# Counting edges behind the samples on ScalarE as sums of signs, and clamping keys on GpSimd, in a graph network on one Trainium2 core

## Chip, cores and metric

The program runs on one core of one Trainium2 chip. A core has five engines that work side by side and wait for each other by semaphores: TensorE (PE; its weight loads are listed as PEld), VectorE (DVE), ScalarE (ACT), GpSimd (POOL) and SyncE (SP), which here issues transfers. The metric is the device time of one execution in microseconds, the median of several. Before the change three runs took 1608.21, 1609.29 and 1603.38 us.

## The reference

Two graph networks follow each other on 6250 nodes with 64 features and 200,000 edges, sorted by destination. Cut to what matters:

```
msg  = x[src]
agg  = segment_sum(msg, dst);  cnt = segment_sum(1, dst)
h    = relu(agg / max(cnt, 1) @ W_l1.T + b_l1 + x @ W_r1.T)
...                                    # the same again with W_l2, b_l2, W_r2
x    = layernorm(x + out)
# three message layers; every node also has an edge to itself with attributes 1
m    = concat([h[dst], h[src], edge_attr]) @ W.T + b
h    = relu(segment_sum(m, dst))       # batch norm and relu after the first two
x    = layernorm(x + h)
```

The destinations are 6250 * u^2 of a uniform u, so low nodes have many more edges than high ones. Each segment sum over gathered rows is a product with the matrix A, where A[d, s] is the number of edges from s to d.

## The kernel before

**Stages.** The kernel builds A once, as 13 tiles of 512 destinations (`TW`) against 6272 padded sources, one byte per element. It multiplies with it in five layers: the first layer while A is being built, and later the second layer and the three message layers, for which the tiles come back from memory. The building takes about the first 540 us of the span. Then come the edge attributes together with the second layer, then the message layers.

**Slots.** A plan made from the expected distribution cuts each tile of A into windows of 1 to 10 destinations and gives each window a number of slots, 2569 in all. A slot is a list of up to 128 edges, one per partition in the product. 128 slots make one row tile t; there are 21 of them. For row tile t the kernel needs the first edge of each of its slots (`start_i[:, t]`, one slot per partition). `fetch(t)` then reads 128 consecutive edges for each slot by two indirect DMAs on the GpSimd queue, one for dst and one for src, into the tile `rows`.

**Keys.** `columns(t)` (lines 900 to 917) turns rows into keys. VectorE takes src >> 7 (L905), combines dst * 49 + (src >> 7) (L906) and src mod 128 (L907), subtracts the first key of the slot's window and takes the minimum with 2000 (L908, the clamp). PE transposes both keys (L913), so that edges lie on partitions and slots along the free dimension, and ScalarE copies them to 16 bits as `k2` (L915). The key of an edge outside the window matches nothing.

**One-hots.** For each 16 slots VectorE writes a one-hot tile `lo` of src mod 128 (128x2048), and for each run of slots a one-hot tile `rhs` of the first key (up to 128x2048). Both are made by the tensor_tensor of L628, which compares `iota` with `k2`, both in SBUF. The pool `hot` holds three buffers of each. PE multiplies lo and rhs slot by slot into PSUM (L1012, tile `pair`, two buffers) and ScalarE writes the finished windows to A as bytes (L1019, L1024). The first layer of a finished tile (`first_layer`; its products are at L666) runs on PE between and beside these products.

**Finding the first edges.** dst is sorted and sampled at every 400th edge (`GAP`); 125 x 4 samples lie in SBUF. The row tiles are searched in five groups (`SEARCH`): tile 0, tiles 1 to 4, 5 to 10, 11 to 15, and 16 to 21; column 21 holds the starts for the attributes. For a group, `near_samples` (L830 to L838) counts the samples below each slot's first destination by a compare on VectorE and a product with ones on PE. `gather_behind` (L843) reads for each row tile of the group the 400 destinations behind the last such sample, one slot per partition, by one indirect DMA on the GpSimd queue into one of six buffers `blks`. `first_edges` (L847 to L864) counts how many of the 400 are below the slot's first destination. This is one tensor_scalar with an accumulator per row tile on VectorE (L852), whose elementwise result `junk` nobody reads. Three more small VectorE instructions for the group (L854, L855, L864) make `start_i` of the counts.

**Order.** `on_slot` (L919 to L950) sets the order of this work within the building loop. At the start of row tile t (slot 32 of tile 0) come `first_edges` of a group whose turn it is (groups 1 to 4 at tiles 0, 2, 4, 6), then `fetch(t + 1)`, then `near_samples` and `gather_behind` of a later group (groups 2 to 4 at tiles 1, 3, 5; group 1 stands before the loop). In the middle of tile t (slot 64; 96 in tile 0) comes `columns(t + 1)`. Instructions marked `pin` keep this order among themselves on their engine. The others are placed by the scheduler of the language by priority and by a model of when their inputs are ready, which is why one-hots stand between the steps of a search on VectorE. Each engine then works through its list in order, and an instruction that waits holds up all that stand behind it on its engine.

GpSimd's list during the building is short: the indirect DMAs of `fetch` (42) and `gather_behind` (22), which it issues itself, and a few memsets. The indirect DMAs of `fetch(t + 1)` can be issued once `start_i` is there and the columns of tile t - 1 have read their buffer of rows, of which there are two.

Of the kernel before, what the change touches and what calls it, by code (L numbers as in the profile page):

```python
# [16 lines left out]
AF = mybir.ActivationFunctionType  # L17
ALU = mybir.AluOpType
# [456 lines left out]
def gnn_kernel(ctx: ExitStack, tc: tile.TileContext, x, src, dst, ea, W_l1, b_l1, W_r1, W_l2, b_l2, W_r2,  # L475
# [10 lines left out]
    nc = tc.nc  # L486
    pin = tc.keep_in_program_order
# [9 lines left out]
    GAP = EC1 // NSMP  # L497
# [26 lines left out]
    c_np = np.zeros((P, 3, R + 1), np.float32)  # L524
# [9 lines left out]
    for i, (b, c, g) in enumerate(subs):  # L534
        e_np[:, 0, i] = E - g * P
        e_np[:, 1, i] = np.arange(P) * g
        e_np[:, 2, i] = b * P
    c_dram = nc.inline_tensor(c_np, name="slot_table")
    e_dram = nc.inline_tensor(e_np, name="attr_table")
    t_dram = nc.inline_tensor(t_np, name="first_edges")  # L540
# [6 lines left out]
    with ExitStack() as fast:  # L547
# [203 lines left out]
        with ExitStack() as bld:  # L751
            ep = bld.enter_context(tc.tile_pool(name="edge", bufs=1))
            tab = ep.tile([P, 3, R + 1], F32, name="tab")
# [16 lines left out]
            most = max(min(b, R + 1) - a for a, b, *_ in SEARCH)  # L770
# [7 lines left out]
            def spare(n):  # L778
                k = free[0].shape[1] - n
                t, free[0] = free[0][:, k:], free[0][:, :k]  # L780
                return t
# [33 lines left out]
            blks = [spare(GAP).bitcast(I32) for _ in range(most)]  # L815
            junk = spare(GAP // 2).bitcast(BF16)
# [5 lines left out]
            c2 = pp.tile([P, R + 1], F32, name="c2")  # L822
# [24 lines left out]
            def first_edges(g):  # L847

                t0, t1 = SEARCH[g][0], min(SEARCH[g][1], R + 1)
                s = slice(t0, t1)  # L850
                for t in range(t0, t1):
                    pin(nc.vector.tensor_scalar(junk, blks[t % most], tab[:, 0, t: t + 1], None,  # L852
                                                ALU.is_lt, ALU.add, accum_out=c2[:, t: t + 1]))
                nc.vector.scalar_tensor_tensor(near[:, s], near[:, s], float(GAP), c2[:, s], ALU.mult, ALU.add)  # L854
                nc.vector.tensor_add(near[:, s], near[:, s], tab[:, 1, s])  # L855
                if g == 0:


                    nc.vector.tensor_single_scalar(near[:, R: R + 1], near[:, s], float(E - P), ALU.min)
                    nc.vector.tensor_copy(start_i[:, s], near[:, R: R + 1])  # L860
                    nc.vector.tensor_sub(near[:, s], near[:, s], near[:, R: R + 1])
                    nc.vector.tensor_scalar(passed, iota[:, :P], near[:, s], 4000.0, ALU.is_lt, ALU.mult)
                else:
                    pin(nc.vector.tensor_copy(start_i[:, s], near[:, s]))  # L864
# [35 lines left out]
            def columns(t):  # L900

                rows = fetched.pop(t)
                hi = ew.tile([P, P], I32, name="hi", bufs=1)
                key = ew.tile([P, 2, P], F32, name="key")
                pin(nc.vector.tensor_single_scalar(hi, rows[:, 1, :], 7, ALU.logical_shift_right))  # L905
                nc.vector.scalar_tensor_tensor(key[:, 0, :], rows[:, 0, :], float(NB), hi, ALU.mult, ALU.add)  # L906
                nc.vector.scalar_tensor_tensor(key[:, 1, :], hi, -float(P), rows[:, 1, :], ALU.mult, ALU.add)  # L907
                nc.vector.tensor_scalar(key[:, 0, :], key[:, 0, :], tab[:, 2, t: t + 1], 2000.0, ALU.subtract, ALU.min)  # L908
                if t == 0:
                    nc.vector.tensor_add(key[:, 0, :], key[:, 0, :], passed)  # L910
                kp = psm.tile([P, 2, P], F32, name="lin")
                for i in range(2):
                    nc.tensor.transpose(kp[:, i, :], key[:, i, :], ident)  # L913
                k2 = ew.tile([P, 2, P, 2], F16, name="k2")
                nc.scalar.copy(k2, kp.unsqueeze(3).to_broadcast([P, 2, P, 2]))  # L915
                cols[t] = k2, {}
                cols.pop(t - 2, None)

            def on_slot(slot):  # L919

                t, c = divmod(slot, P)
                if c == (32 if t == 0 else 0):
                    for g, (*_, t1) in enumerate(SEARCH):
                        if t == t1:
                            first_edges(g)
                            if g == len(SEARCH) - 1:
                                first_attributes()
                    if t + 1 < R:
                        fetch(t + 1)
                    for g, (_, _, t0, _) in enumerate(SEARCH):  # L930
                        if t == t0:
                            near_samples(g)
                            gather_behind(g)
                    gather_dst(t)
                if c == (96 if t == 0 else 64) and t + 1 < R:
                    columns(t + 1)
                    if t == 0:
                        for to, of in early_weights:
                            transposed(to, of)
# [13 lines left out]
            gather_behind(0)  # L953
            near_samples(1)
            first_edges(0)
            fetch(0)
            gather_behind(1)
            columns(0)
            load_x()
            pin(nc.sync.dma_start(thr[:, early:], t_ap[:, early:].to_broadcast([EP, P * (R + 1) - early])))  # L960
# [331 lines left out]
```

## Time and profile before

The profile shows one execution. Its own time was 1605.75 us, of which the span from the program's first instruction to its last is 1604.0 us. The mean granted clock of TensorE was 0.977.

| engine | busy, us | share of the span |
|---|---|---|
| PE | 1488.1 | 93% |
| PEld | 1370.7 | 85% |
| DVE | 905.4 | 56% |
| ACT | 575.4 | 36% |
| POOL | 217.7 | 14% |

The groups of instructions around the change:

| line, engine | what | count | us of one |
|---|---|---|---|
| L852 DVE | count among 128x400, int32 to bf16, with accumulator | 22 | 0.62 |
| L908 DVE | subtract and minimum on 128x128 f32 | 21 | 0.28 |
| L906, L907 DVE | the two keys | 21 each | 0.29 |
| L628 DVE | one-hots rhs (240) and lo (161) | 401 | 1.02 and 1.22 |
| L843 POOL | indirect DMA into blks | 22 | 0.94 to 10.95 |
| L896 POOL | indirect DMA into rows | 42 | 0.94 to 22.88 |
| L1019 ACT | evacuation of pair | 355 | 0.90 |

How to read the profile: busy times are those of the whole span, while the engines are busy in different stages, so a stage is judged by the slices and windows of that stage. The chain of waits is followed back from the last instruction, at each step to what released it. "Idle before" is the time for which an engine stood still ahead of a group, with what ended most of it. For an indirect DMA the record on POOL is the time in which GpSimd issues it, not that of the transfer, which lands later.

### The profile page before, as it was taken

Reading aid. Unit: us, or ns where it says so; the run is one execution under the profiler, and the core shown is the slowest. Engines: PE = TensorE matmul, PEld = TensorE weight load, DVE = VectorE, ACT = ScalarE, POOL = GpSimd, SP = SyncE. Lnnn points to the kernel's source line nnn. Section 1 sums busy time; section 2 is a strip of 40 time slices with the busy share of each in tenths; the row PEclk is TensorE's granted clock in tenths of the full one; section 3 lists DMA queues with packets and bytes.
Section 4 is the critical chain, followed back from the end, with each engine's and each line's share of the span. In section 5 each row is a group of like instructions: output and inputs, shape, how many; then the busy total and the mean of one; then the engine's idle time right before and its main releaser. Section 6 shows DMA issues by size and latency. Waiting matters only on the chain.

```text
span 1604.0 us, 38502 instructions
## 1 busy us (share of the span) xinstructions
PE 1488.1 (93%) x17115; PEld 1370.7 (85%) x17115; DVE 905.4 (56%) x1499; ACT 575.4 (36%) x1086; POOL 217.7 (14%) x93
## 2 busy tenths in 40 slices
PE   3887799999998999999999999999899999999997
PEld 2666688888886898899899989889799999899997
DVE  5899998988968509987986511111431112442222
ACT  2737476777848404544553200000310000310000
POOL 2465830731601100000000000000000000000000
PEclk9898999999999999999999999999899999899998
DMA  5302232320421536435344354443345444164540
GB/s 135 125 29 96 46 100 88 154 99 4 169 85 71 226 160 243 174 131 200 135 146 148 135 241 161 162 171 122 132 167 220 177 175 168 81 247 173 197 163 11
DMA packets 45200, 227.32 MB, mean 142 GB/s; under 512 B 23621, under 2 KB 31650, under 8 KB 37343
## 3 DMA queue, kind: packets, MB, share of 16 engines
q1 hardware_dynamic: 37965, 139.40, 23.1%
q10 hardware_dynamic: 4306, 78.10, 12.4%
q0 software_dynamic: 2752, 7.26, 1.6%
q8 instruction: 136, 2.23, 0.5%
q14 instruction: 41, 0.34, 0.1%
HBM read 183.77 MB, written 42.57 MB: 141 GB/s over the span
## 4 chain that ended last, share of the span: by engine, by line
PE 65%; DVE 17%; issue 7%; ACT 6%; DMA 3%; POOL 2%; ACTq 0%; DVEq 0%; POOLq 0%
PE agg L666 49%; PE pair L1012 7%; DVE lo L628 6%; ACT a L1019 3%; DVE rhs L628 2%; PE u L1166 2%; POOL parts L843 2%; DVE e L1070 2%; PE bank L1079 1%; DVE z L693 1%; DMA e<-in_edge_attr_dram 1%; DVE e L1072 1%; PE lin L1188 1%; PE tr L718 1%; PE lin L740 1%
## 5 line engine op out<-in xcount | busy, mean ns | idle before, releaser
L666 PE MATMUL agg<-parts,a 128*128 128x192 bf16 (+1 forms) x12005 | 1088.2, 247 | 4.4 <-DVE parts L649 1.3
L666 PEld LDWEIGHTS <-a 128*128 128x128 fp8e3 x12005 | 1006.4, 98 | 30.5 <-issue 19.6
L1019 ACT ACTIVATE a<-pair 128x784 fp8e3<-128x784 f32 (+3 forms) x355 | 294.2, 900 | 106.2 <-PE pair L1012 90.4
L1012 PE MATMUL pair<-rhs,lo 128*128 128x147 bf16 (+5 forms) x2569 | 259.4, 237 | 43.7 <-ACT a L1019 17.0
L1012 PEld LDWEIGHTS <-lo 128*128 128x128 bf16 x2569 | 191.6, 100 | 97.6 <-issue 49.2
L628 DVE TENSOR_TENSOR rhs<-iota,k 128x1960 bf16<-128x1960 f16 (+15 forms) x240 | 239.5, 1020 | 18.5 <-ACT k L915 10.5
L628 DVE TENSOR_TENSOR lo<-iota,k 128x2048 bf16<-128x2048 f16 x161 | 195.7, 1220 | 1.9 <-ACT k L915 1.3
L693 DVE TENSOR_REDUCE z<-agg 128x256 f32<-128x768 f32 (+1 forms) x39 | 35.3, 910 | 271.8 <-PE agg L666 271.4
L896 POOL DMA_INDIRECT rows<-ends,start_i x40 | 140.4, 3510 | 180.3 <-DVE key L908 154.1
L628 DVE TENSOR_TENSOR lo<-iota,e_d 128x2048 bf16<-128x2048 f16 (+11 forms) x132 | 130.9, 1012 | 19.6 <-PE bank L1079 17.6
L1079 PE MATMUL bank<-lo,lhs 128*128 128x128 bf16 x1701 | 107.6, 219 | 17.6 <-ACT lhs L1073 12.4
L1079 PEld LDWEIGHTS <-lhs 128*128 128x128 bf16 x1701 | 98.3, 98 | 29.1 <-ACT lhs L1073 20.4
L693 DVE TENSOR_REDUCE nd<-agg 128x256 f32<-128x768 f32 (+1 forms) x26 | 23.5, 907 | 116.5 <-PE agg L666 110.8
L1182 POOL TENSOR_TENSOR nd<-res,inv 128x256 f32<-128x256 f32 (+1 forms) x13 | 7.6, 588 | 550.2 <-DVE z L1128 341.2
L720 ACT COPY mx<-tr 128x512 f32<-128x512 f32 (+1 forms) x26 | 14.7, 566 | 169.7 <-PE tr L718 169.6
L709 ACT ACTIVATE sp_r<-z 128x256 f32<-128x256 f32 (+1 forms) x26 | 10.5, 403 | 172.2 <-DVE z L708 172.0
L1206 ACT ACTIVATE hr<-hr 64x512 f32<-64x512 f32 (+1 forms) x13 | 7.9, 605 | 172.2 <-DVE hr L1205 172.2
L843 POOL DMA_INDIRECT parts<-in_dst_dram,pos x22 | 53.9, 2448 | 41.0 <-DVE pos L838 31.6
L1069 ACT CAST lhs<-e 128x512 bf16<-128x512 f32 (+21 forms) x72 | 36.1, 503 | 64.0 <-PE bank L1079 43.4
L1070 DVE TENSOR_TENSOR e<-e,lhs 128x512 f32<-128x512 f32 (+21 forms) x72 | 39.5, 552 | 14.9 <-ACT lhs L1069 14.7
L1191 DVE TENSOR_SCALAR ext<-lin 64x512 f32<-64x512 f32 (+1 forms) x13 | 8.6, 663 | 68.5 <-ACT hr L1189 68.5
L1073 ACT CAST lhs<-e 128x512 bf16<-128x512 f32 (+21 forms) x72 | 36.4, 505 | 23.1 <-DVE e L1072 22.6
(149 smaller groups left out, 816.4 us busy)
## 6 DMA issues: line engine op xcount, KB each, us to landing
a<-adj SPq DMA_DIRECT2D x24, 3136.0 KB
a<-adj ACTq DMA_DIRECT2D x24, 3136.0 KB
adj<-a SPq DMA_DIRECT2D x12, 3136.0 KB
e<-in_edge_attr_dram SPq DMA_DIRECT2D x25, 256.0 KB
a<-adj SPq DMA_DIRECT2D x4, 784.0 KB
out_dram<-z SPq DMA_DIRECT2D x12, 128.0 KB
e<-in_edge_attr_dram SPq DMA_DIRECT2D x7, 152.0 KB
adj<-a SPq DMA_DIRECT2D x1, 784.0 KB
```

What stands on the lines that cost most here:

```text
L628: nc.vector.tensor_tensor(to.rearrange("p g (h two) -> p g h two", two=2), iota[:, :n].rearrange("p (h two) -> p h two", two=2).unsqueeze( ...
L666: nc.tensor.matmul(sums[k][:, i, :n], views[k][:, b, i * P: (i + 1) * P], pt[:, b, :n], start=(b == sources[0] and terms is None and not ( ...
L693: nc.vector.tensor_reduce(to, ps[:, :nb, : 3 * D].rearrange("p b (r d) -> p b d r", r=3), AX.X, ALU.add)
L843: pin(nc.gpsimd.indirect_dma_start(out=blks[t % most], out_offset=None, in_=dst.rearrange("(e o) -> e o", o=1), in_offset=bass.IndirectOff ...
L896: pin(nc.gpsimd.indirect_dma_start(out=rows[:, i, :], out_offset=None, in_=end, in_offset=bass.IndirectOffsetOnAxis(ap=start_i[:, t: t + 1 ...
L1012: nc.tensor.matmul(pair[:, bank % 2, col: col + wc], lo_hot(t, c), rhs[:, i, :wc], start=first, stop=last)
L1019: nc.scalar.activation(av[:, :, o: o + 2 * nd].rearrange("p h (two d) -> p h two d", two=2), pair[:, :, : nd * NB].rearrange("p two (d h) ...
L1069: nc.scalar.copy(lhs[:, :g, 0:EC], r)
L1070: nc.vector.tensor_sub(r, r, lhs[:, :g, 0:EC])
L1073: nc.scalar.copy(lhs[:, :g, 2 * EC:3 * EC], r)
L1079: nc.tensor.matmul(ps[:, :P], lhs[:, q, :], oh[:, q % HOT, :], start=(c == 0 and q == 0), stop=(i == last_b[b] and q == g - 1))
L1166: pin(nc.tensor.matmul(u[:, i, :], y[:, i * P: (i + 1) * P], maps[n - 1], start=True, stop=True))
```

## The change

In `first_edges` the counts of groups 1 to 4 (21 instructions) move from VectorE to ScalarE. ScalarE has no compare with a sum, so it takes the sign of (threshold - destination) for each of the 400 destinations and accumulates the signs. To keep the difference from ever being zero, the thresholds in the table `c_np[:, 0]` are lowered by 0.5. The sum is (number below) - (number above), so (sum + 400) / 2 is the count, and one more VectorE instruction per group makes it. Group 0 keeps its count on VectorE.

In `columns` the clamp of the first key moves from VectorE to GpSimd for all row tiles but tile 0 (20 instructions). It now stands on GpSimd between VectorE's L906 and PE's transposes.

```diff
@@ -535,6 +535,7 @@
         e_np[:, 2, i] = b * P
+    c_np[:, 0] -= 0.5
     c_dram = nc.inline_tensor(c_np, name="slot_table")
...
@@ -849,8 +850,15 @@
                 for t in range(t0, t1):
-                    pin(nc.vector.tensor_scalar(junk, blks[t % most], tab[:, 0, t: t + 1], None,
-                                                ALU.is_lt, ALU.add, accum_out=c2[:, t: t + 1]))
+                    if g == 0:
+                        pin(nc.vector.tensor_scalar(junk, blks[t % most], tab[:, 0, t: t + 1], None,
+                                                    ALU.is_lt, ALU.add, accum_out=c2[:, t: t + 1]))
+                    else:
+
+                        pin(nc.scalar.activation(junk, blks[t % most], AF.Sign, bias=tab[:, 0, t: t + 1], scale=-1.0,
+                                                 accum_out=c2[:, t: t + 1]))
+                if g:
+                    nc.vector.tensor_scalar(c2[:, s], c2[:, s], float(GAP), 0.5, ALU.add, ALU.mult)
                 nc.vector.scalar_tensor_tensor(near[:, s], near[:, s], float(GAP), c2[:, s], ALU.mult, ALU.add)
...
@@ -905,7 +913,7 @@
                 nc.vector.scalar_tensor_tensor(key[:, 1, :], hi, -float(P), rows[:, 1, :], ALU.mult, ALU.add)
-                nc.vector.tensor_scalar(key[:, 0, :], key[:, 0, :], tab[:, 2, t: t + 1], 2000.0, ALU.subtract, ALU.min)
+                (nc.gpsimd if t else nc.vector).tensor_scalar(key[:, 0, :], key[:, 0, :], tab[:, 2, t: t + 1], 2000.0, ALU.subtract, ALU.min)
                 if t == 0:
```

## The prediction

> **What bounds the kernel now.** I read the page first: its slices of 40 us, then the chain of waits.
>
> ```profile
> PE   3887799999998999999999999999899999999997
> ...
> DVE  5899998988968509987986511111431112442222
> ...
> PE 65%; DVE 17%; issue 7%; ACT 6%; DMA 3%; POOL 2%; ACTq 0%; DVEq 0%; POOLq 0%
> ```
>
> TensorE sets the end over most of the span, but not everywhere: in slices 1 to 4 (40 to 200 us) PE reads 8877 and DVE 8999. The change touches only the building of adjacency tiles, which fills these slices, so I cut them into windows of 20 us.
>
> ```profile
> core 0: us, PE busy (x) PEld busy (x) DVE busy (x) ACT busy (x) POOL busy (x), PEclk, DMA share, GB/s
> ...
> 80.00:100.00 20.00, 19.67 (x302) 17.21 (x300) 20.00 (x35) 4.05 (x6) 6.79 (x2) 1.00 0.01 3
> 100.00:120.00 20.00, 14.53 (x124) 10.31 (x123) 20.00 (x34) 8.14 (x16) 18.01 (x7) 0.91 0.18 55
> 120.00:140.00 20.00, 13.10 (x149) 9.40 (x147) 19.89 (x30) 19.22 (x25) 2.69 (x2) 1.00 0.04 11
> ```
>
> DVE is full from about 60 to 210 us. There a microsecond off VectorE's queue is a microsecond off the end, as long as PE's idle time lasts: windows 20 to 200 us hold 141.7 us of PE in 180, so about 38 us can be won at most. From 200 to 440 us PE is busy 231.6 of 240 us and hides small VectorE savings.
>
> **What VectorE gets rid of.** The timeline of DVE around the first moved count:
>
> ```profile
> 30.28 0.62 DVE L852 TENSOR_SCALAR_CACHE_REDUCE parts<-parts,tab 128x400 bf16<-128x400 int32 x1
> 30.83 0.08 DVE L852 DVE_READ_ACCUMULATOR parts<-parts,tab 128x1 f32 x1
> 30.83 1.22 DVE L628 TENSOR_TENSOR lo<-iota,k 128x2048 bf16<-128x2048 f16 x1
> ```
>
> A count costs 0.55 us from start to start. 22 counts less the one of group 0 leaves 21: 21 x 0.55 = 11.6 us, all between 30 and 169 us. The clamp L908 costs 0.20 from start to start (48.02 to 48.22). 20 move, 4.0 us; ten of them (tiles 2 to 9, 12, 16) stand where DVE has no gap, 2.0 us; the rest was hidden behind PE. DVE also waited 1.34 us at 159.33 for a gather; that wait goes to ACT. Added: four small tensor_scalars on c2, 0.07 each by L837 (58.16 to 58.23), 0.3. Gain 11.6 + 2.0 + 1.3 - 0.3 = **14.6 us**.
>
> **What ScalarE gets.** No row shows a Sign or an accumulator on ACT. The nearest with a bias are L742 (678 ns at 512 from PSUM) and L1163 (759 at 512, bias and scale). At 0.9 ns an element, the slope between L1024 at 490 elements (0.58) and at 392 (two in 0.98, 0.49 each), 400 elements are 0.58 to 0.66; with DVE's 0.08 for the accumulator about 0.7, so 21 x 0.7 = 15 us. ACT is 53% busy from 60 to 200 us and PE waits only 7.9 us for its evacuations L1019, so I take 2 us, ends 0 and 10. If Sign needs its own table, each group pays two loads of 1.28 us (the row of L915): 0 to 10 us, I take 0. Queued behind a Sign that waits for its gather are the evacuations of pair, and PE behind them. In group 1 the extra c2 step lengthens the way to start_i by one hop (36.89 to 38.04 to 39.25): 1 us, ends -3 and 3, the gain being that ACT may count earlier.
>
> **What GpSimd gets.** Free of others it is cheap, L552 being the nearest row, against 0.28 on DVE. The chance of it being free is what decides. Timelines of POOL and of DVE:
>
> ```profile
> 1.95 0.54 POOL L552 TENSOR_SCALAR minus<-ident 128x128 bf16<-128x128 f32 x1
> ...
> 59.80 1.61 POOL L843 DMA_INDIRECT parts<-in_dst_dram,pos  x1 [12.55 <-DVE pos L838]
> ...
> 95.23 9.20 POOL L843 DMA_INDIRECT parts<-in_dst_dram,pos  x1 [0.29 <-DVE pos L838]
> 104.73 7.76 POOL L843 DMA_INDIRECT parts<-in_dst_dram,pos  x1 [0.30 <-issue]
> ...
> 141.92 10.95 POOL L843 DMA_INDIRECT parts<-in_dst_dram,pos  x1 [18.77 <-DVE pos L838]
> ...
> 235.25 1.88 POOL L896 DMA_INDIRECT rows<-ends,start_i  x1 [14.25 <-DVE key L908]
> ...
> 291.26 22.88 POOL L896 DMA_INDIRECT rows<-ends,start_i  x1 [20.93 <-DVE key L908]
> ```
>
> ```profile
> 103.51 0.29 DVE L908 TENSOR_SCALAR key<-key,tab 128x128 f32<-128x128 f32 x1
> ...
> 151.96 0.29 DVE L908 TENSOR_SCALAR key<-key,tab 128x128 f32<-128x128 f32 x1
> ...
> 313.23 0.29 DVE L908 TENSOR_SCALAR key<-key,tab 128x128 f32<-128x128 f32 x1
> ```
>
> The same gather takes 0.94 us on a quiet chip and up to 22.88 while DVE runs one-hots back to back. It is not the DMA: three of the long ones end at 104.43, 152.87 and 314.14, each 0.91 to 0.92 us after the start of a **DVE clamp**, as if begun only then; 173.16 and 401.91 do the same (clamps at 188.36, 416.23). Others end after a count, a read of PSUM (L729) or a gap. So POOL's read of SBUF is shut out by the one-hots (two SBUF inputs), and what let it in were the counts and clamps that the change takes off VectorE. At 59.80 and 235.25 the wait was one one-hot only, so it is not certain each time.
>
> The Trainium skill ("SBUF — State Buffer", § Who interferes with whom) says that a VectorE instruction with two SBUF inputs contends with a GpSimd instruction that reads SBUF, and that the second to issue blocks until the first has finished. Taken literally that is one one-hot, at most 1.2 us a clamp, hidden behind the finished one-hots, which gives the first rival's time; this trace shows 22 us across some 18 one-hots, and I go by the trace.
>
> Who waits for the clamp? PE's two transposes L913, in order, with all later matmuls behind them. From the end of the clamp to the transposes tiles 1, 2, 4, 5, 7 and 16 have 0.06 us, and 3, 8, 9, 12 and 20 under 0.9; 6, 10, 11, 13 to 15 and 17 to 19 have 2.3 to 15.1, which hides the move (where it is gone, the price is that of a plain tile below). A shut-out clamp is released when DVE runs out of lo and rhs buffers (3 each); by the ends of the matmuls that last read them they are free about 4 us before they are written again, from 80 to 140 us. Then DVE idles for clamp 0.54, a hop 0.15 (48.29 to 48.35 is 0.06, taken twice and rounded up), transposes 0.44 and 10 to 13 matmuls of 0.1 until a buffer is free, 1.3: **2.5 us**.
> - Plain tiles 1, 3, 5, 7, 8, 9, 12, 16, 20: ends 0 and 2.5 each. After one stall PE runs late and the next key is early for it, so I take half: 9 x 1.2 = 11 (0 to 22).
> - Tiles 2, 4, 6: the clamp of tile t+1 stands on POOL behind the 6, 5 and 6 gathers issued at tile t's start, 1.25 apart when free (18.20 to 19.45), and behind fetches whose rows are early enough. Tile 2: gathers end at 68.19, key was at 66.55: 2.5. Tile 4: gather one is shut out as at 95.23, five follow in DVE's idle time, 5 x 1.25 + 2.5 = 8.8. Tile 6: 6 x 1.25 + 2.5 = 10, less 2.3 slack, 8. Together 19 (0 if let in, 25).
>
> A granted POOL instruction can hold VectorE in turn:
>
> ```profile
> 480.86 5.33 POOL L979 MEMSET a<- 128x6272 int32 x1 [32.94 <-PE pair L1012]
> ...
> 481.73 4.48 DVE L730 TENSOR_SCALAR inv<-cnt 128x4 f32<-128x4 f32 x1
> ```
>
> L730 is 0.16 elsewhere. A clamp let in early may so cost DVE its 0.54 for the 0.20 saved, 10 x 0.3 = 3 us in the rival; in the forecast it runs while DVE is idle.
>
> **Sum.** The profiled execution took 1605.75 us (span 1604.0 and 1.75 around it), 2.5 below the median 1608.21 and inside the runs' 1603.38 to 1609.29; I start from it. -14.6 + 11 + 19 + 2 + 1 = +18: **1624 us**.
>
> **Rivals.** *POOL is let in at the next boundary* (59.80, 235.25 speak for it; the five ends on L908 against): no stall, gain 14.6, less 3 held DVE and 1 to 3 for ACT and the chain: 1595. It decides as soon as the clamp waits under about 4 us, DVE's lead in buffers, and the gathers are through before it. *Gain and stalls cancel*: clamps get in, but the gathers of tiles 4 and 6 still stand in front, 14.6 - 3 against 12 to 14: 1606. For it: these gathers were slow already. *ACT becomes the bound* (19.22 of 20 at 120 to 140 us): table loads 10 and blocked evacuations 10 instead of 2, on top of the forecast: 1642. Against it: ACT idles 106 us before L1019.
>
> **How the numbers follow.** Forecast 0.56, let in 0.26, cancel 0.12, ACT 0.06. A measurement here tells about 0.5% from no change, so faster is below 1600, slower above 1616. The forecast's own range is 1610 (no plain stall, gathers 19) to 1650 (22 + 25 + 10 for ACT + 3 for the chain), each less 14.6; but for its lowest edge, which I leave with it, it is slower: slower 0.62, same 0.12, faster 0.26. The range reaches down past 1595 to 1591, the lower ends, and up to 1650: 1591 to 1650.
>
> **What would show it.** POOL clamps with a median over 1 us and some over 4; waits of L913's transposes for the key (5.4 us before) of 20 us or more, then named POOL; DVE gaps of 2 us or more before L628, released by PE, between 80 and 210 us; gaps of 8 us near the gathers of tiles 4 and 6. Wrong if clamps stay near 0.5 us, if POOL runs them ahead of the gathers, or if DVE has no gaps and the spans shift left by 10 us at 210. A table load next to each Sign would show the third rival.

## Result and the profile after

The change makes the kernel slower: 1647.5 us in the median of four runs, against 1605.8 us in four runs of the kernel before, a ratio of 1.027 (95% interval 1.024 to 1.030). That is about 42 us more, where the prediction had 18 more. The direction came as predicted, GpSimd's read is shut out as predicted, and the time lies in the range (1591 to 1650). What such a wait costs was priced wrongly, and the gathers and the gain were mis-sized too.

The profiled execution took 1645.6 us with a span of 1643.7, 39.7 more than before. The change puts eight lines into the kernel, so the clamp is L916 after, the transposes L921, the fetch L904, the Sign L858, the one-hots L629 and the products of slots L1020. First the slices of 40 us, the chain and the group of the clamp, all of the kernel after:

```profile
PE   3677789899898889999999999999899999999997
DVE  5779978997877723997888721111341211441222
PE 53%; DVE 10%; issue 4%; DMA 3%; ACT 3%; POOL 1%; SPq 0%; ACTq 0%; POOLq 0%; DVEq 0%
L916 POOL TENSOR_SCALAR key<-key,tab 128x128 f32<-128x128 f32 x20 | 62.9, 3145 | 299.3 <-DVE key L914 236.2
```

VectorE is less full in slices 1, 2 and 5, counted from 0 as in the prediction (7, 7 and 7; before 8, 9 and 9), as if it had been relieved. But PE is less full there too (6, 7 and 8; before 8, 8 and 9). The clamp, 0.28 us on VectorE, takes 3.1 us in the mean on GpSimd. PE's waits during the building show who pays; first the kernel before (20 to 540 us), then the kernel after (20 to 577 us, where its building ends). The columns are the total, the number of waits and the longest:

```profile
PE pair L1012 <- ACT a L1019: 17.0, 46, 0.7
PE pair L1012 <- DVE lo L628: 12.8, 20, 2.1
PE pair L1012 <- DVE rhs L628: 7.5, 14, 1.1
PE lin L913 <- DVE key L908: 2.2, 1, 2.2
```

```profile
PE lin L921 <- POOL key L916: 40.8, 11, 6.0
PE pair L1020 <- ACT a L1027: 19.0, 45, 1.4
PE pair L1020 <- DVE lo L629: 7.0, 9, 2.1
PE pair L1020 <- DVE rhs L629: 4.5, 7, 2.0
```

PE waits 8.8 us less for one-hots (20.3 to 11.5) and 38.6 us more for keys. One of these waits in full, tile 8, in the timelines of VectorE, of GpSimd and of PE's weight loads after:

```profile
197.92 0.28 DVE L915 SCALAR_TENSOR_TENSOR key<-hi,rows 128x128 f32<-128x128 int32 x1
198.13 1.15 DVE L629 TENSOR_TENSOR rhs<-iota,k 128x1924 bf16<-128x1924 f16 x1
199.20 1.22 DVE L629 TENSOR_TENSOR lo<-iota,k 128x2048 bf16<-128x2048 f16 x1
200.33 1.16 DVE L629 TENSOR_TENSOR rhs<-iota,k 128x1924 bf16<-128x1924 f16 x1
201.40 1.22 DVE L629 TENSOR_TENSOR lo<-iota,k 128x2048 bf16<-128x2048 f16 x1
204.48 0.24 DVE L629 TENSOR_TENSOR rhs<-iota,k 128x148 bf16<-128x148 f16 x1 [1.86 <-PE pair L1020]
```

```profile
198.18 5.03 POOL L916 TENSOR_SCALAR key<-key,tab 128x128 f32<-128x128 f32 x1 [13.67 <-DVE key L914]
```

```profile
203.26 0.29 PEld L921 LDWEIGHTS lin<-ident,key 128*128 128x128 f32 x2 [5.03 <-POOL key L916]
```

The clamp's record starts at 198.18. VectorE makes four more one-hots, until its buffers are full, and the last one ends at 202.62. The clamp ends 0.59 us later, at 203.21, and PE goes on at 203.26, having stood for 5.03 us. VectorE itself stood for 1.86. So **PE loses the whole time in which VectorE fills its buffers, not only VectorE's own pause after it**: the one-hots made meanwhile belong to products that stand behind the transposes in PE's list.

The building ends at 576.6 instead of 539.9, 36.7 us later. PE's busy time up to there grows by 7.2 of these (466.3 to 473.5), and its idle time by the other 29.5. The granted clock of the stretch falls from 0.96 to 0.93, and a product of a slot takes 242 ns instead of 237. That the clock makes the 7.2 is not shown: in the run with three openings below, the clock of the building is 0.94 and PE's busy time 465.7. Three more us come after it, most of them where the second layer waits for the first tile of A to come back from memory (1.1 us before, 3.6 after).

### The profile page after: what moved, and what is told of

It reads as the page before. It is cut to its first block, busy times and chain, and to the rows that moved or that the text cites. A ratio compares the mean times of both kernels' runs of the same rounds, so it can differ in the third digit from the quotient of the medians.

```text
span 1643.7 us, 38531 instructions
## 1 busy us (share of the span) xinstructions
PE 1495.7 (91%) x17115; PEld 1384.7 (84%) x17115; DVE 893.9 (54%) x1441; ACT 587.1 (36%) x1128; POOL 164.9 (10%) x113
## 4 chain that ended last, share of the span: by engine, by line
PE 53%; DVE 10%; issue 4%; DMA 3%; ACT 3%; POOL 1%; SPq 0%; ACTq 0%; POOLq 0%; DVEq 0%
PE agg L667 44%; DVE lo L629 4%; DMA e<-in_edge_attr_dram 2%; PE pair L1020 2%; PE u L1174 2%; PE bank L1087 2%; DVE e L1078 1%; DVE z L694 1%; DVE e L1080 1%; DMA a<-adj 1%; PE lin L1196 1%; ACT a L1027 1%; PE lin L1195 1%; POOL key L916 1%; PE tr L719 1%
## 5 line engine op out<-in xcount | busy, mean ns | idle before, releaser
L1020 PE MATMUL pair<-rhs,lo 128*128 128x147 bf16 (+5 forms) x2569 | 265.6, 242 | 35.9 <-ACT a L1027 19.0
L1020 PEld LDWEIGHTS <-lo 128*128 128x128 bf16 x2569 | 199.8, 103 | 81.6 <-issue 48.1
L629 DVE TENSOR_TENSOR rhs<-iota,k 128x1960 bf16<-128x1960 f16 (+15 forms) x240 | 240.2, 1020 | 49.9 <-PE pair L1020 31.8
L629 DVE TENSOR_TENSOR lo<-iota,k 128x2048 bf16<-128x2048 f16 x161 | 195.9, 1221 | 12.5 <-PE pair L1020 10.4
L629 DVE TENSOR_TENSOR lo<-iota,e_d 128x2048 bf16<-128x2048 f16 (+11 forms) x132 | 131.0, 1013 | 19.7 <-PE bank L1087 17.7
L916 POOL TENSOR_SCALAR key<-key,tab 128x128 f32<-128x128 f32 x20 | 62.9, 3145 | 299.3 <-DVE key L914 236.2
L921 PE MATMUL lin<-ident,key 128*128 128x128 f32 x42 | 10.9, 344 | 54.1 <-POOL key L916 40.8
L1077 ACT CAST lhs<-e 128x512 bf16<-128x512 f32 (+21 forms) x72 | 36.1, 503 | 63.7 <-PE bank L1087 40.5
L921 PEld LDWEIGHTS lin<-ident,key 128*128 128x128 f32 x42 | 5.4, 165 | 56.8 <-POOL key L916 43.4
L904 POOL DMA_INDIRECT rows<-ends,start_i x40 | 49.2, 1230 | 28.4 <-DVE start_i L872 17.1
```

The source lines that it names most:

```text
L629: nc.vector.tensor_tensor(to.rearrange("p g (h two) -> p g h two", two=2), iota[:, :n].rearrange("p (h two) -> p h two", two=2).unsqueeze( ...
L904: pin(nc.gpsimd.indirect_dma_start(out=rows[:, i, :], out_offset=None, in_=end, in_offset=bass.IndirectOffsetOnAxis(ap=start_i[:, t: t + 1 ...
L916: (nc.gpsimd if t else nc.vector).tensor_scalar(key[:, 0, :], key[:, 0, :], tab[:, 2, t: t + 1], 2000.0, ALU.subtract, ALU.min)
L1020: nc.tensor.matmul(pair[:, bank % 2, col: col + wc], lo_hot(t, c), rhs[:, i, :wc], start=first, stop=last)
L1077: nc.scalar.copy(lhs[:, :g, 0:EC], r)
```

## Experiments

Line numbers in these kernels are shifted by a few; the operands name the instructions. Each time is compared with the kernel before on the chip of that run: 1607.8, 1613.3 or 1605.1 us on the three chips. Waits are compared with the profile of the kernel before that is shown above, also where the chip is another.

**The counts alone.** The kernel after with the clamp back on VectorE, L916:

```diff
-                (nc.gpsimd if t else nc.vector).tensor_scalar(key[:, 0, :], key[:, 0, :], tab[:, 2, t: t + 1], 2000.0, ALU.subtract, ALU.min)
+                nc.vector.tensor_scalar(key[:, 0, :], key[:, 0, :], tab[:, 2, t: t + 1], 2000.0, ALU.subtract, ALU.min)
```

> Counts of groups 1 to 4 on ScalarE, clamp on VectorE as before. Port theory (GpSimd's clamp is shut out by VectorE's one-hots and PE stands behind it; this makes the whole loss): faster than before by 8 to 15 us, ratio 0.991 to 0.995, PE's wait for the key at the transposes near 5 us as before. ScalarE theory (the signs and accumulator reads, 21 x 0.82 us, hold up the evacuations of pair): slower than before by 10 us or more, PE's waits for ScalarE's evacuations up by as much.

1604.5 us against 1607.8, ratio 0.998 (0.997 to 0.999): a gain of 3.3 us, less than the 8 to 15 expected. Its waits of PE for one-hots from 20 to 533 us, and a wait of the second layer:

```profile
PE pair L1020 <- DVE lo L629: 8.4, 10, 2.1
PE pair L1020 <- DVE rhs L629: 4.9, 9, 0.8
```

```profile
PE agg L667 <- DMA a<-adj: 4.3, 1, 4.3
```

The waits for one-hots fall by 7.0 us (20.3 to 13.3) and the building ends 7.2 us earlier (532.7). At the second layer 3.2 us of it are lost to the transfer of the first tile, 4.3 us instead of 1.1: what is early there waits for memory.

**The clamp alone.** The kernel before with the clamp on GpSimd, so the edit above the other way round, in the kernel before.

> Clamp of tiles 1 to 20 on GpSimd, all counts on VectorE as before. Port theory: slower than before by 40 to 60 us (the change's 42 and what the counts had won), GpSimd's clamp with a median over 2 us, PE's wait for the key 35 us or more. ScalarE theory: within 10 us of before. If the counts on VectorE are openings for GpSimd that matter, the clamps of tiles 3, 5 and 7, which follow counts, are shorter than the 6.0, 1.8 and 1.8 us of the changed kernel.

1650.6 us, ratio 1.027 (1.024 to 1.029), as much as the whole change. Here the building ends at 581.0. PE's idle time before the transposes, of which 45.4 us are waits for the key (40.8 in the whole change):

```profile
L913 PE MATMUL lin<-ident,key 128*128 128x128 f32 x42 | 10.7, 346 | 57.9 <-POOL key L908 45.4
```

The loss is the clamp's. That the counts matter as openings for GpSimd does not show: the clamps of tiles 3, 5 and 7 took 6.02, 6.17 and 0.87 us with the counts on VectorE, and 6.02, 1.76 and 1.79 without.

**A clamp that nobody reads.** The kernel before with an extra clamp on GpSimd, behind the clamp on VectorE:

```diff
                 nc.vector.tensor_scalar(key[:, 0, :], key[:, 0, :], tab[:, 2, t: t + 1], 2000.0, ALU.subtract, ALU.min)
+                if t:
+                    nc.gpsimd.memset(idle, 0.0)
+                    nc.gpsimd.tensor_scalar(idle, key[:, 0, :], tab[:, 2, t: t + 1], 2000.0, ALU.subtract, ALU.min)
```

> The kernel before, with two instructions more on GpSimd for each tile from 1 on: a memset of a 128x128 scratch tile (writes only) and the same clamp once more into that tile, which nobody reads. Port theory: the memset takes the same 0.2 to 0.3 us each time, the unread clamp between 0.5 and over 10 us, longest where VectorE runs one-hots without a gap, and it ends soon after VectorE comes to an instruction of one SBUF input or stands; the kernel's time stays within 1% of before, as PE waits for neither. A theory that GpSimd's arithmetic itself is slow: 2 us or more each time, also beside an idle VectorE. A theory that GpSimd's list or the wait for VectorE's signal is what is late: the records of the clamp stay near 0.5 us.

One run took 1639.4 us, 2% above the kernel before: the expectation of no loss was wrong. The memset, which only writes, always took 0.22 to 0.23 us; the clamp took 0.71 to 20.87. The longest in GpSimd's timeline, with what stood behind it, and VectorE's wait for it from 20 to 540 us:

```profile
296.24 20.87 POOL L912 TENSOR_SCALAR idle<-key,tab 128x128 f16<-128x128 f32 x1 [18.94 <-DVE key L909]
317.38 1.03 POOL L897 DMA_INDIRECT rows<-ends,start_i  x1 [0.27 <-issue]
```

```profile
DVE hi L906 <- DMA rows<-ends,start_i: 28.8, 4, 10.5
```

Nobody reads the clamp, but the fetch of the next rows stands behind it in GpSimd's list, comes late, and VectorE then waits for the rows: 28.8 us in four waits, where the kernel before has 4.2 in two. The building ends 26.6 us later (566.5). During the 20.87 us VectorE's full one-hots took 1.17 and 1.22 us, as elsewhere. This shows the shut-out, but one run does not tell whether a shut-out read costs anything beyond the late rows.

**One opening.** The kernel after with a short VectorE instruction of one SBUF input, 64 elements, pinned behind the second key:

```diff
+                if t:
+                    pin(nc.vector.tensor_scalar(idle, ident[:, :64], tab[:, 2, t: t + 1], 2000.0, ALU.subtract, ALU.min))
```

> The changed kernel, with one VectorE instruction more for each tile from 1 on: right behind the second key, a subtract and minimum of 64 elements of the constant identity (one SBUF input) into a scratch tile that nobody reads. Port theory: it opens the port at the moment GpSimd's clamp is waiting; clamps fall to a median under 1.2 us, PE's wait for the key from 43 us to under 15 us, and the kernel is faster than the changed one by 25 to 45 us although VectorE has 20 instructions more. Any theory in which GpSimd's clamp is slow by itself or stands behind its list: no change, or slower by 2 to 3 us.

1654.3 us, ratio 1.029 (1.025 to 1.033): no help, as the theories with a slow clamp expected. VectorE and GpSimd at tile 3:

```profile
85.86 0.27 DVE L920 TENSOR_SCALAR idle<-ident,tab 128x64 f32<-128x64 f32 x1
86.05 1.21 DVE L629 TENSOR_TENSOR lo<-iota,k 128x2048 bf16<-128x2048 f16 x1
```

```profile
85.90 6.12 POOL L918 TENSOR_SCALAR key<-key,tab 128x128 f32<-128x128 f32 x1 [13.03 <-DVE key L915]
```

The opening is there at 85.86, the clamp's record starts at 85.90, and the next one-hot at 86.05. The opening came as the clamp was only starting, in this tile and in most others, so this run decides nothing.

**Three openings.** The same with three such instructions. The scheduler set one-hots between them, so that they became three separate openings, about 1.2 us apart:

```diff
+                for _ in range(3 if t else 0):
+                    pin(nc.vector.tensor_scalar(idle, ident[:, :64], tab[:, 2, t: t + 1], 2000.0, ALU.subtract, ALU.min))
```

> The kernel after, with three short VectorE instructions of one SBUF input (64 elements a partition, result unread) pinned right behind the second key of tiles 1 to 20, so that no one-hot starts for about half a us while GpSimd's clamp wants to read. The earlier opening of one such instruction ended about when the clamp's record began. Theory (one-hots with two SBUF inputs shut GpSimd's read out until VectorE does something else): the clamp's median falls from 2.74 us to under 1.2, PE's waits for the key from 43 to under 20 us, and the time falls by 20 to 35 from the kernel after, to 1612 to 1627. Rival (GpSimd's clamp is long for a reason of its own, such as its start-up or its semaphore): the clamp keeps 2 us or more and the time stays within 8 us of the kernel after.

1617.6 us against 1613.3 for the kernel before on this chip, ratio 1.003 (1.001 to 1.005): by the time nine tenths of the loss are gone, with clamp and counts where the change put them and 60 instructions more on VectorE. By the profile the building ends at 551.6, which is 25.0 of the 36.7 us; why the time gained more than that stays open. PE's waits for the key from 20 to 552 us, then tile 9 on VectorE and GpSimd:

```profile
PE lin L925 <- POOL key L918: 17.7, 11, 3.0
```

```profile
211.98 0.25 DVE L920 TENSOR_SCALAR idle<-ident,tab 128x64 f32<-128x64 f32 x1
212.14 1.16 DVE L629 TENSOR_TENSOR rhs<-iota,k 128x1924 bf16<-128x1924 f16 x1
213.21 0.37 DVE L920 TENSOR_SCALAR idle<-ident,tab 128x64 f32<-128x64 f32 x1
213.50 1.15 DVE L629 TENSOR_TENSOR rhs<-iota,k 128x1924 bf16<-128x1924 f16 x1
```

```profile
212.03 1.86 POOL L918 TENSOR_SCALAR key<-key,tab 128x128 f32<-128x128 f32 x1 [17.26 <-DVE key L915]
```

The clamp starts at 212.03, misses the first opening, waits through one one-hot, and ends at 213.89, 0.68 us after the second opening began; that one is stretched from 0.25 to 0.37. In 19 of 20 tiles the clamp ends 0.58 to 0.76 us after the start of such an instruction. One opening is not always enough: in tiles 6, 8 and 13 one that began 0.35 to 1.18 us after the start of the clamp's record let it wait on, and only the next let it in. Eight clamps of the kernel after took over 3 us, one does here. The median fell to 1.83 us, not under 1.2 as expected, since mostly the second opening and not the first lets it in. A start-up of GpSimd's own would not follow VectorE's short instructions like this; that rival is out. Whether the one input of these instructions matters or only that they are short, no run separates.

**The clamp on ScalarE.** The kernel after, with ScalarE for the clamp (`upper` holds 2000 + base):

```diff
-                (nc.gpsimd if t else nc.vector).tensor_scalar(key[:, 0, :], key[:, 0, :], tab[:, 2, t: t + 1], 2000.0, ALU.subtract, ALU.min)
+                nc.vector.tensor_scalar(key[:, 0, :], key[:, 0, :], tab[:, 2, t: t + 1], 2000.0, ALU.subtract, ALU.min) if t == 0 else \
+                    nc.scalar.activation(key[:, 0, :], key[:, 0, :], AF.Relu, bias=upper[:, t: t + 1], scale=-1.0)
...
+                    nc.scalar.activation(k2[:, 0], kp[:, 0, :].unsqueeze(2).to_broadcast([P, P, 2]), AF.Identity, bias=most_t, scale=-1.0)
+                    nc.scalar.copy(k2[:, 1], kp[:, 1, :].unsqueeze(2).to_broadcast([P, P, 2]))
```

> The kernel after, with the clamp of tiles 1 to 20 on ScalarE instead of GpSimd: ScalarE computes Relu(2000 + base - key), which is 2000 minus the clamped key, and turns it back when it copies the transposed key to 16 bits, so that the same keys result; the copy of both keys becomes two instructions. Both the clamp and its place off VectorE stay, only the engine differs. Theory (GpSimd's read is shut out by the one-hots and PE stands for about 5 us at each such key): the clamp on ScalarE takes under 0.7 us each however busy VectorE is, PE's waits for the key stay under 15 us in all against 43 after, and the time is 1595 to 1610. Rival (any trip of the key off VectorE costs PE a wait, because the key is on the path): waits for the key stay above 25 us, time 1625 to 1645. Rival (ScalarE becomes the bound through its queue): waits of PE for ScalarE's evacuations grow from 17 us to over 35, time above 1615.

1614.4 us against 1613.3, ratio 1.001 (0.999 to 1.003). The clamps take 0.38 to 0.47 us each. PE's waits from 20 to 550 us:

```profile
PE pair L1029 <- ACT a L1036: 29.7, 53, 4.0
PE pair L1029 <- DVE lo L629: 5.2, 8, 1.7
PE pair L1029 <- DVE rhs L629: 4.5, 6, 1.3
```

The waits for the key are gone (0.4 us, in one), so it is not the trip off VectorE that costs, but GpSimd's read. In their place the waits for the evacuations grow from 17.0 to 29.7 us: ScalarE's queue takes back what VectorE gave, 20.3 - 9.7 = 10.6 us. The theory was right on the clamps and the waits for the key, but not on the time of 1595 to 1610. The first rival is out; the second expected over 35 us of waits for evacuations, and was half right.

**An unread read behind the fetch.** The kernel before with one unread GpSimd clamp of a constant tile per row tile, pinned behind the two indirect DMAs of the next rows and behind the gathers:

```diff
+                    if t + 1 < R:
+                        pin(nc.gpsimd.tensor_scalar(idle, ident, tab[:, 2, t: t + 1], 2000.0, ALU.subtract, ALU.min))
```

> The kernel before (clamp and counts on VectorE) with one more GpSimd instruction per row tile, an unread clamp of a constant 128x128 tile, pinned behind the two indirect DMAs of the next rows and behind the gathers of that place, so that nothing urgent of the same row tile stands behind it and PE waits for nothing of it. It tells where the 32 us of the unread clamp ahead of the fetch came from. Theory (a shut-out read costs only what stands behind it on GpSimd or waits for it): its records are again 0.7 to 20 us long, VectorE's busy time is unchanged, and the time is within 8 us of the kernel before. Rival (the waiting read itself slows VectorE or holds it once granted): the time is 15 to 35 above the kernel before, with one-hots longer than 1.02 and 1.22 us on average or VectorE held beside the reads.

1605.7 us against 1613.3, ratio 0.996 (0.995 to 0.998). There is no loss, so the rival is out: the waiting read does not slow VectorE (one-hots 1.02 and 1.22 us, as before). Only one of the 20 reads took over 2.5 us here; in the second timing below three took 6.0 to 10.6, at a ratio of 1.001. GpSimd's timeline at row tiles 11 and 17:

```profile
240.03 1.75 POOL L936 TENSOR_SCALAR idle<-ident,tab 128x128 f16<-128x128 f32 x1
...
419.16 10.65 POOL L936 TENSOR_SCALAR idle<-ident,tab 128x128 f16<-128x128 f32 x1
```

The expected 0.7 to 20 us were 0.71 to 10.65, with a median of 1.35. At 240.03 VectorE runs one-hots without a pause and the read still gets in after about one of them; the one-hot beside it, at 241.20, takes 1.31 us instead of 1.22. At 419.16 it waits through nine, and also past a one-input instruction of 4 elements (a reciprocal at 420.27, 0.17 us). What decides between the two stays open.

**Is the small gain real?** Added work that nobody needs cannot be expected to make a kernel faster, and here it seemed to. So this kernel and the one with the counts alone were timed again, on one chip.

> The kernel with the counts on ScalarE and the clamp back on VectorE, timed again next to the kernel with the unread GpSimd instruction behind the fetches, on one chip. The first gave 0.9979 and the second, which only adds work, 0.9961, each on its own chip. If the gain of the counts is real, this kernel is below the kernel before by 0.1 to 0.4% again and below the other of this pair by about as much. Rival: differences of this size come from the placing of transfers in time alone (the profiled executions wait between 1 and 6 us for the first tile of A to come back); then the two are within 0.2% of each other.

> The kernel before with the unread GpSimd instruction behind the fetches, timed again. If the gain of the counts is real and this one's was chance, this comes within 0.1% of the kernel before. Rival (differences of this size tell nothing of the added or moved work): below the kernel before by 0.2 to 0.4% again.

The counts alone: 0.998 (0.997 to 1.000), 1603.0 us against 1605.1. The unread read: 1.001 (1.000 to 1.003), 1608.3 us. The first gain came again at about its size and the second did not. The counts on ScalarE are worth some 2 to 3 us, hardly more than can be told from nothing: the unread read's first interval (0.995 to 0.998) lay clear of 1 too, and that gain did not come again. The profiled execution again ended the building early (8.0 us, at 531.9) and again lost 3 us to the first tile of A (4.1 us instead of 1.1). No version that was tried beat the kernel before by more than that twice.

## Why the prediction was right in kind and wrong in size

By its own steps, up to the end of the building:

| step | predicted, us | measured, us |
|---|---|---|
| what VectorE gets rid of | -14.6 | -8.8 (waits for one-hots 20.3 to 11.5) |
| plain tiles 1, 3, 5, 7, 8, 9, 12, 16, 20 | +11 | +31.0 (PE's added waits for the key) |
| tiles 2, 4, 6 with gathers | +19 | +8.8 (4.8, 3.6, 0.4) |
| ScalarE's queue | +2 | +2.0 (waits for evacuations 17.0 to 19.0) |
| the chain of the search in group 1 | +1 | 1.6 (VectorE's three waits for a Sign, all groups) |
| PE's own busy time | not in it | +7.2 (cause open) |

The waits by tile are those of PE's weight loads, after less before. The rows are readings of different queues and need not add up to the 36.7 us by which the building ends later. They add to 41.8; that the others are covered elsewhere was not traced further.

**The step that failed is the price of a plain tile**, "**2.5 us**" and then "so I take half: 9 x 1.2 = 11". The first half of it is what the runs show: the one-hots shut GpSimd's read out, and where PE stood longest it got in when VectorE stopped for want of buffers. Nine of the 20 clamps ended 0.58 or 0.59 us after VectorE fell idle, among them those of tiles 3, 8, 9, 12, 16 and 20; five others got in between two one-hots. But the step charged VectorE's idle time. It is PE that stands, from the moment when it reaches the transposes, through up to four one-hots until the buffers are full, and then through the clamp: 5.0 us at tile 8, 6.0 at tile 3, 5.3 at tile 9. Nor did one stall make the next one half as dear: tiles 5 and 7 added only 1.0 and 0.0, but tiles 8, 9, 12, 16 and 20 added 5.0, 5.3, 3.2, 4.4 and 4.7. The 31.0 us are 3.4 a tile instead of 1.2.

The gather term erred the other way. At tile 4 the first gather was expected to be shut out again as in the kernel before (9.20 and 7.76 us); it took 1.99, and the next 1.89 and 1.84:

```profile
103.70 1.99 POOL L844 DMA_INDIRECT parts<-in_dst_dram,pos  x1 [0.81 <-issue]
```

VectorE made no pause for them. It ran one-hots without a gap from 103.22 to 109.13, and each of the three got in as soon as the one-hot that was running had ended, as the prediction's first rival has it; why here and not in the kernel before stays open. The fetches shrank from 140.4 us to 49.2 in all: each pair now stands behind a clamp that has done the waiting. (The 22.88 us that the prediction gives for "the same gather" are a fetch; the gathers' longest was 10.95.) No gap of 8 us appeared; the longest wait of these tiles was 5.1.

The gain was taken one for one from VectorE's list. But what the list can give to the end is what PE waits for it, 20.3 us in the whole building and not the 38 us of PE's idle time from 20 to 200 us that the prediction named as the ceiling; 10.2 of these were waits for evacuations. So 12.6 us off VectorE's list (the counts and the wait for a gather, less the added steps) moved the end of the building by 7.2, and the end of the program by 3.3 and 2.1 in two measurements.

That the time lies in the range is partly luck. The plain tiles cost more than the 22 us of their upper end; the range had room for them because it also held 25 us for the gathers and 10 for ScalarE, of which 8.8 and 2.0 came. (The upper end adds up to 1651, not 1650.)

Signs that came as said: the median of the clamps 2.74 us, the longest 6.10; the waits of the transposes' weight loads for the key 43.4 us (5.4 before), now named GpSimd; VectorE's waits for PE before one-hots up to 4.8 us. The three rivals are out: POOL was let in between two one-hots in five of 20 clamps, which is not often enough, gain and stalls did not cancel, and ScalarE did not become the bound. Its table loads are two after as before, at 6.6 and about 655 us, none of them at a Sign.

The Trainium skill ("SBUF — State Buffer", § Who interferes with whom) has the pair of instructions right, and the write-only memset at 0.22 us beside the clamp agrees with it. That the second one waits only until the first finishes (same page, § 🎯 Summary: rules for kernel authors) does not agree in full: it is too short for the 20.87 us above, and right for the 1.75 us at 240.03. Another page ("Perfetto Trace Analysis", § Optimizing Scalar/DVE Operations) warns that moving work between these two engines might not help, because they share a read port; here the clamp's move cost about 42 us.

## What to carry to other kernels

Charge a delayed input to the engine that stands for it, for as long as it stands, and not to the engine whose buffers ran full; in a list worked off in order, work made in the meantime helps nobody. A saving on a busy engine is worth at most the waits for that engine on the one that sets the end. Work on GpSimd that reads SBUF beside two-input VectorE instructions belongs where nothing urgent stands behind it, or needs short one-input instructions after its start to let it in.

## What the runs showed of the hardware

- A VectorE instruction of 64 elements with one SBUF input let a waiting GpSimd read in most of the time: the clamp ended 0.58 to 0.76 us after the start of one in 19 of 20 tiles, though in three tiles one more had gone by. The instruction itself was stretched from 0.25 to at most 0.37 us.
- A shut-out read costs VectorE nothing while it waits; one-hots keep 1.02 and 1.22 us on average. When it gets in, the one-hot beside it takes up to 0.1 us longer (1.31 instead of 1.22). Whether it waits through one (1.75 us) or through some 18 of them (20.87) no run here explains.
- A Sign with a sum of 400 elements takes 0.63 us on ScalarE and the reading of its accumulator 0.19 more, against 0.62 and 0.08 for the compare on VectorE.
